# A kernel whose builder searches for its own instruction order: eight series of rounds in place of one

## The chip, the cores and the metric

The kernel runs on one core of a Trainium2 chip. The metric is the time in microseconds on the device. Before the change the median of three runs is 3045.0 us (3042.98 to 3045.96).

An order of instructions is fixed when the program is built. The time that the builder takes on the host is not part of the metric.

## The reference

The input is 64 graphs of 256 nodes with 256 features, and an adjacency matrix of 0 and 1 for each. Four layers follow one another; each normalizes, computes, and adds to `x`.

```python
h = jnp.maximum(_layernorm(x), 0.0); x = x + gat0(h, adj)   # layer 0
h = jnp.maximum(_layernorm(x), 0.0); x = x + gat1(h, adj)   # layer 1
h = jnp.maximum(_layernorm(x), 0.0); x = x + gat2(h, adj)   # layer 2
h = jnp.maximum(_layernorm(x), 0.0); x = x + ggnn(h, adj)   # layer 3
# gat0, gat1: 4 heads of 64; gat2: one head of 256
Wh = h @ W;  e = leaky_relu(Wh @ a_src [:, None] + Wh @ a_dst [None, :])
out = softmax(where(adj > 0, e, NEG)) @ Wh       # gat0: elu(out)
                                                 # gat1: relu(out + bias) + Wh, layer norm per head
# ggnn: three steps of a gated recurrent unit (GRU)
m = h @ weight[i];  aggr = adj.T @ m
r, z = sigmoid(aggr @ w_ih.T + h @ w_hh.T + b), ...;  n = tanh(i_n + r * h_n)
h = (1 - z) * n + z * h
```

## The kernel before

**Units.** The 64 graphs are cut into 33 units: graph 0 alone (unit 0), 31 pairs (units 1 to 31), graph 63 alone (unit 32). For each unit, `graphs` records the four layers as operations: `layer0`, `layer1`, `layer2`, `gru`. Nothing is issued at this point. Before the units comes a group of set-up work, numbered -1: loads of weights, score columns, the products of the GRU's input weights (`input_gates`, line 1033), and differences of weights that are stored to DRAM as `sd` (line 1073) and read back as `sw` by every pair in every GRU step (line 1611).

**What the lines in the profile are.** The attention layers use TensorE for transposes (line 1144), projections (1166), the spreading of scores in the first three units (1203) and the weighted sums (1275). The attention weights `pt` are made by ScalarE (1256) and VectorE; the latter goes through the helper at line 913, as most VectorE work does. `layer1` then has a chain of some ten VectorE steps for each half of the heads, with a power on GpSimd in it (1408, 1409) and the addition onto `xt` (1420). `norm` has statistics on VectorE (1109, 1110), a power on GpSimd (1118, 1119) and ScalarE's `xn` or `hn` (1127). The GRU has aggregations over the adjacency matrix (1471), products for pairs (1623, 1566), gates (1486) and transposes back (1501). SyncE issues the loads (1320, 1322), four DMA transposes of the mask per pair (1352), the broadcast of scores (1230), the `sw` loads (1611) and the stores (1703).

**Who sets the order.** `_Schedule` (from line 546 of the kernel) does. Each recorded operation has an engine, a cost in ns, the operations that it needs, and the buffers that it takes from pools of fixed size (5 of `xt`, 13 of `g`, 3 of `sw`, 8 PSUM banks and so on). Three of its methods matter here.

- `paths` gives every operation a first due time. It counts back from the end of the operation's unit, which lies at half of `PACE` = 93800 ns for each graph up to the unit's last.
- `play(due)` plays the program forward by the costs. An engine that is free takes, of the operations that have all they need, the one due first:

```python
heapq.heappush(able[o.engine], (due[o.index], o.index))
```

  It also gives out the buffers. It returns the order with its planned start times, the buffers taken, and the planned span.
- `latest(starts)` plays the program backward from the end, taking the operations in the reverse of the planned starts. What it returns is how late each operation could start; that is the next round's due times.

`run` lets `play` and `latest` alternate for seven rounds and keeps the order with the shortest planned span. It then issues every operation in that order, and each engine executes its instructions in the order issued. The same operations are issued whatever the order; what differs is their sequence on each engine, the buffers that they get, and so the waits between engines.

The costs stand in the code: for example 1725 for a GRU product of a pair, `dve(700)` less an overlap of 80 for a VectorE operation on 512 elements per partition, 485 less 80 for one on `pt`, 450 for any DMA issued by SyncE, 340 from TensorE's end to the start of another engine. `play` has one TensorE speed.

Of the kernel before, what the change touches and what calls it, by code (L numbers as in the profile page):

```python
# [2 lines left out]

# [542 lines left out]
class _Schedule:  # L546
# [11 lines left out]

    ENGINES = ("pe", "act", "dve", "pool", "sp")
    OVERLAP = {"pe": 0, "act": 90, "dve": 80, "pool": 0, "sp": 0}
    HOP = {"pe": 340, "act": 210, "dve": 210, "pool": 240, "sp": 0}
# [2 lines left out]
    DMA_AHEAD = 2000  # L566
    STRETCH = 3.43
    MARGIN = 1100
    ROUNDS = 7

    def __init__(self, tc, pools):

# [91 lines left out]
    def latest(self, starts):  # L664

        left = {o.index: len(o.succs) for o in self.ops}
        able = {e: [] for e in self.ENGINES}
        idle = dict.fromkeys(self.ENGINES, True)
        events, before_end = [], {}
# [8 lines left out]
        while True:  # L678
            for e in self.ENGINES:
                held = []  # L680
# [31 lines left out]
    def play(self, due):  # L712

        ops = self.ops
        able = {e: [] for e in self.ENGINES}
        idle = dict.fromkeys(self.ENGINES, True)
        waits = [len(o.preds) for o in ops]
# [26 lines left out]
        while True:  # L744
            for e in self.ENGINES:
                if not idle[e] or e == "sp" and dma_free > clock + self.DMA_AHEAD:
# [42 lines left out]
        return trace, slots, clock if done == len(ops) else float("inf")  # L789

    def run(self):
        due = self.paths()
        self.span = float("inf")
        for _ in range(self.ROUNDS):
            trace, slots, span = self.play(due)
            if span < self.span:
                self.trace, taken, self.span = trace, slots, span
            elif span == float("inf"):
                break
            due = self.latest({o.index: clock for clock, o in trace})  # L800
        assert self.span < float("inf")
        for _, o in self.trace:
            for b in o.takes:
                if b.tile is None:
                    b.slot = taken[b]
                    b.tile = self.pools[b.cls][0].tile(b.shape, b.dtype, name=f"{b.cls}{b.slot}")
            self.issue(o)
# [980 lines left out]
```

## Time and profile before

| what | value |
|---|---|
| median of the runs | 3045.0 us |
| the profiled execution | 3046.62 us |
| its span, first to last instruction | 3044.8 us |
| TensorE busy | 2974.3 us (98%) |
| TensorE loading weights | 2478.7 us (81%) |
| VectorE busy | 2606.7 us (86%) |
| ScalarE busy | 2124.8 us (70%) |
| GpSimd busy | 425.4 us (14%) |
| mean granted TensorE clock | 0.991 |

The profile is of one execution. "Busy" is the time in which an engine had an instruction under way. A view by windows cuts the span into stretches and gives the busy time of each engine in each, the granted TensorE clock and the DMA's share. A view of waits gives, for each engine, the time that it sat idle before instructions of a line, and which instruction let it go on. A timeline lists the instructions of one engine in order; what stands in square brackets is the idle time before the instruction and who ended it. An fp32 matmul is recorded as two.

### The profile page before, as it was taken

The numbers are of one execution on the slowest core, as the hardware profiler recorded it, in microseconds if no ns is written. First come the engines' busy times: TensorE is split into PE (matmuls) and PEld (weight loads), VectorE is DVE, ScalarE is ACT, GpSimd is POOL, SyncE is SP. The second block draws the span as 40 slices with busy tenths as digits, with TensorE's granted clock in tenths as the row PEclk, the third lists the DMA queues.
The fourth block names the chain that finished last, engine by engine and source line by source line (L and its number), as shares of the span: only waits on it lengthen the run. The fifth ranks groups of instructions, "written<-read, shape, count | busy, mean of one in ns | idle before, by whom it ended". The sixth has DMA issues, their size and how long they took to land.

```text
span 3044.8 us, 58325 instructions
## 1 busy us (share of the span) xinstructions
PE 2974.3 (98%) x21458; PEld 2478.7 (81%) x21458; DVE 2606.7 (86%) x6310; ACT 2124.8 (70%) x4997; POOL 425.4 (14%) x643
## 2 busy tenths in 40 slices
PE   8699999999999999999999999999999999999998
PEld 7588787888888888888888888888888888888887
DVE  7877788988988888988888988888988888988774
ACT  7566577776777776677777777777777777776554
POOL 3301101111111011111011111011111011111000
PEclk9799999999999999999999999999999999999999
DMA  5111122212212212212222222211222221211110
GB/s 146 40 62 44 55 81 78 81 54 84 74 64 84 84 54 80 74 65 83 84 67 69 72 67 84 84 70 64 70 70 81 84 72 62 67 63 59 49 42 28
DMA packets 150946, 212.56 MB, mean 70 GB/s; under 512 B 49238, under 2 KB 102012, under 8 KB 143228
## 3 DMA queue, kind: packets, MB, share of 16 engines
q1 hardware_dynamic: 146752, 207.40, 21.3%
q8 instruction: 172, 2.82, 0.4%
q10 hardware_dynamic: 3900, 1.34, 0.2%
q14 instruction: 122, 1.00, 0.1%
HBM read 180.62 MB, written 19.68 MB: 66 GB/s over the span
## 4 chain that ended last, share of the span: by engine, by line
PE 90%; DVE 6%; ACT 1%; DMA 1%; POOL 1%; SPq 1%; issue 0%; ACTq 0%; DVEq 0%; POOLq 0%
PE bank L1623 34%; PE bank L1486 12%; PE bank L1166 11%; PE bank L1275 11%; PE bank L1566 9%; PE bank L1471 6%; PE bank L1144 4%; PE bank L1501 3%; DVE o L913 1%; DVE g L913 1%; DVE pt L913 1%; SPq L1352 1%; PE bank L1203 1%; DMA sw<-sd 1%; ACT pt L1256 1%; DVE mean L913 0%
## 5 line engine op out<-in xcount | busy, mean ns | idle before, releaser
L913 ACT ACTIVATE g<-bank,bg 128x256 f32<-128x256 f32 (+1 forms) x780 | 395.3, 522 | 222.0 <-PE bank L1623 100.1
L1256 ACT ACTIVATE pt<-cb,f 128x256 f32<-128x256 f32 x1062 | 465.0, 504 | 99.9 <-PE bank L1275 99.6
L913 DVE SCALAR_TENSOR_TENSOR pt<-pt,f,cap 128x256 f32<-128x256 f32 x1152 | 487.7, 477 | 18.1 <-ACT pt L1256 12.8
L1275 PEld LDWEIGHTS bank<-wh,pt 128*64 128x64 f32 (+1 forms) x8704 | 347.7, 141 | 73.5 <-issue 46.7
L1275 PE MATMUL bank<-wh,pt 128*64 128x65 f32 (+1 forms) x8704 | 396.0, 232 | 7.5 <-DVE pt L913 6.7
L1486 PE MATMUL bank<-ag,wc 128*128 128x512 f32 (+1 forms) x888 | 383.1, 561 | 0.0
L913 ACT ACTIVATE g<-g,bg 128x256 f32<-128x256 f32 x570 | 267.1, 502 | 133.3 <-DVE g L913 105.2
L1623 PE MATMUL bank<-g,sw 128*128 128x256 f32 x1488 | 351.5, 379 | 0.0
L913 ACT COPY g<-bank 128x512 f32<-128x512 f32 x279 | 163.1, 585 | 252.0 <-PE bank L1623 234.3
L1623 PEld LDWEIGHTS bank<-g,sw 128*128 128x128 f32 x1488 | 282.7, 190 | 38.6
L1486 PEld LDWEIGHTS bank<-ag,wc 128*128 128x128 f32 x888 | 160.6, 190 | 106.9 <-issue 95.4
L1118 POOL TENSOR_SCALAR mv<-mv 128x4 f32<-128x4 f32 (+1 forms) x132 | 48.0, 364 | 1409.9 <-DVE mv L1110 1131.3
L1471 PE MATMUL bank<-am_r,hl 128*128 128x256 f32 x1536 | 235.1, 299 | 0.8 <-DVE am_r L913 0.4
L913 DVE TENSOR_TENSOR g<-bank,g 128x512 f32<-128x512 f32 x279 | 190.3, 683 | 37.4 <-PE bank L1623 20.7
L1127 ACT ACTIVATE xn<-xt,mv 128x256 f32<-128x256 f32 x384 | 208.9, 598 | 10.9 <-DVE mv L913 10.5
L1109 DVE BATCH_NORM_STATS2 st<-xt 128x6 f32<-128x256 f32 x512 | 208.6, 407 | 7.7 <-DMA xt<-in_x_dram 7.4
L1471 PEld LDWEIGHTS bank<-am_r,hl 128*128 128x128 f32 x1536 | 202.4, 189 | 10.6 <-DVE hl L913 1.1
L1623 PE MATMUL bank<-ag,sw 128*128 128x256 f32 x744 | 179.1, 384 | 7.7 <-DVE g L913 4.1
L1623 PE MATMUL bank<-ag,wc 128*128 128x256 f32 x744 | 179.4, 384 | 0.7 <-ACT ag L913 0.7
L1623 PE MATMUL bank<-ht,whh 128*128 128x256 f32 x744 | 178.7, 384 | 0.8 <-ACT ht L913 0.8
L1623 PE MATMUL bank<-g,s 128*128 128x256 f32 x744 | 176.1, 380 | 0.0
L1623 PE MATMUL bank<-g,wc 128*128 128x256 f32 x744 | 175.9, 379 | 0.0
(128 smaller groups left out, 5892.7 us busy)
## 6 DMA issues: line engine op xcount, KB each, us to landing
sw<-sd SPq DMA_DIRECT2D x279, 256.0 KB, 2.6
cb<-rd SPq DMA_DIRECT2D x58, 1024.0 KB, 4.6
xt<-in_x_dram SPq DMA_DIRECT2D x31, 512.0 KB, 3.7
at<-in_adj_dram SPq DMA_DIRECT2D x31, 512.0 KB, 6.0
out_dram<-xt SPq DMA_DIRECT2D x31, 512.0 KB, 3.0
cb<-rd SPq DMA_DIRECT2D x29, 256.0 KB, 3.3
sd<-g SPq DMA_DIRECT2D x9, 256.0 KB, 2.3
cap<-cap_n SPq DMA_TRANSPOSE x128, 2.4
```

Of the source, the lines that this page charges most:

```text
L913: emit = lambda: fn(*[a() if callable(a) else a for a in args], **kw)
L1109: nc.vector.bn_stats(st.tile[:, c, :], xt.tile[:, c, :])
L1127: op("act", 610, lambda: nc.scalar.activation(xn.tile[:, c, :], xt.tile[:, c, :], AF.Relu, bias=mv.tile[:, 3, c : c + 1], scale=mv.tile[:, ...
L1144: nc.tensor.transpose(ps.tile[:, c * P : (c + 1) * P], xn.tile[:, c, dc * P : (dc + 1) * P], ident)
L1166: nc.tensor.matmul(ps.tile[:, : heads * W], lhsT=ht.tile[:, dc, c * P : (c + 1) * P], rhs=we[:, dc].rearrange("p h w -> p (h w)"), start=( ...
L1256: op("act", 500, lambda: nc.scalar.activation(pt.tile[:, b, jc, :], source(h, b), AF.Exp, scale=slope - 1.0, bias=f.tile[:, 1, h, c : c + ...
L1275: nc.tensor.matmul(ps[q * Q : (q + 1) * Q], lhsT=pt.tile[:, b, jc, i0 : i0 + Q], rhs=wh.tile[:, h, 2 * b + jc, :w], start=(jc == 0), stop= ...
L1471: nc.tensor.matmul(ps.tile[:, b * N : (b + 1) * N], lhsT=hl.tile[:, k, 2 * b + sc, :], rhs=am.tile[:, 2 * b + sc, :], start=(k == 0 and sc ...
L1486: nc.tensor.matmul(ps.tile[:, :S], lhsT=w[:, dc, g * P : (g + 1) * P], rhs=v.tile[:, dc, :], start=(first and dc == 0), stop=(last and dc ...
L1501: nc.tensor.transpose(ps.tile[:, c * P : (c + 1) * P], ht.tile[:, j, c * P : (c + 1) * P], ident)
L1566: op("pe", 432, lambda: nc.tensor.matmul(ps.tile[:, where], lhsT=w, rhs=v(), start=first, stop=False, skip_group_check=True,), [*reads, B_ ...
L1623: nc.tensor.matmul(ps.tile[:, j * N : (j + 1) * N], lhsT=w()[:, dc, j * P : (j + 1) * P], rhs=view()[:, dc], start=(first and j == 0 and d ...
```

## The change

`run` searches in `KICKS` = 8 series of up to `ROUNDS` = 4 rounds each, in place of one series of seven. The first series starts from `paths`, as before. Each later series starts from `home`, the due times derived from the best order so far, with an offset added to whole groups: each group with a number below 6 is moved with a chance of 0.6, by an amount drawn from a normal distribution with a deviation of 30000 ns. Number -1 is below 6 as well, so the set-up work is among the groups that can move. The random numbers come from a fixed seed, so that the build always gives the same order. The order with the shortest planned span over all the series is issued.

```diff
+import random
...
-    ROUNDS = 7
+    ROUNDS = 4
+    KICKS = 8
+    SEED = 13
+    SHAKE = 30000.0
...
     def run(self):
-        due = self.paths()
+        home, close = self.paths(), float("inf")
         self.span = float("inf")
-        for _ in range(self.ROUNDS):
-            trace, slots, span = self.play(due)
-            if span < self.span:
-                self.trace, taken, self.span = trace, slots, span
-            elif span == float("inf"):
-                break
-            due = self.latest({o.index: clock for clock, o in trace})
+        rnd = random.Random(self.SEED)
+        groups = sorted({o.group for o in self.ops})
+        for kick in range(self.KICKS):
+
+            off = {g: rnd.gauss(0, self.SHAKE) if kick and g < 6 and rnd.random() < 0.6 else 0.0 for g in groups}
+            due = {o.index: home[o.index] + off[o.group] for o in self.ops}
+            for _ in range(self.ROUNDS):
+                trace, slots, span = self.play(due)
+                if span == float("inf"):
+                    break
+                due = self.latest({o.index: clock for clock, o in trace})
+                if span < close:
+                    home, close = due, span
+                if span < self.span:
+                    self.trace, taken, self.span = trace, slots, span
         assert self.span < float("inf")
```

No operation, cost, pool or dependency is touched.

## The prediction

> **What bounds the kernel now.** I read the page's first two parts, then the windows, then TensorE's waits in the stretch that the windows pointed to, then timelines of TensorE and SyncE. The page:
>
> ```profile
> span 3044.8 us, 58325 instructions
> PE 2974.3 (98%) x21458; PEld 2478.7 (81%) x21458; DVE 2606.7 (86%) x6310; ACT 2124.8 (70%) x4997; POOL 425.4 (14%) x643
> PE   8699999999999999999999999999999999999998
> PEclk9799999999999999999999999999999999999999
> ```
>
> TensorE is the bound: it idles 3044.8 - 2974.3 = 70.5 us. Of 40 slices only the first three and the last are below 9, and the granted clock drops in the second. Cut by stage (columns: span, then busy time and instructions of PE, PEld, DVE, ACT, POOL, then clock, DMA share, GB/s):
>
> ```profile
> 0.00:80.00 80.00, 65.66 (x718) 57.18 (x720) 58.04 (x184) 60.39 (x175) 23.25 (x49) 1.00 0.48 139
> 80.00:145.00 65.00, 41.02 (x376) 34.12 (x373) 54.78 (x162) 31.57 (x76) 20.54 (x25) 0.76 0.15 45
> 145.00:360.00 215.00, 201.99 (x1407) 170.17 (x1406) 170.57 (x422) 137.58 (x328) 33.26 (x46) 0.96 0.18 56
> 360.00:500.00 140.00, 135.58 (x1033) 111.44 (x1032) 118.50 (x291) 104.98 (x254) 17.06 (x26) 0.99 0.22 68
> 500.00:2960.00 2460.00, 2454.24 (x17568) 2042.16 (x17567) 2161.89 (x5170) 1754.85 (x4092) 330.05 (x495) 1.00 0.22 71
> 2960.00:3045.00 85.00, 75.80 (x372) 63.57 (x370) 42.94 (x89) 35.43 (x78) 1.21 (x2) 0.98 0.09 27
> ```
>
> Idle by stage: 14.3, 24.0, 13.0, 4.4, 5.8, 9.2 us. From 500 to 2960 us it is 0.2%: no order can win anything there, but one could lose. The start, 80 to 500, holds 41.4 us. The first 14.3 are nearly all the wait for the first input: the first matmul starts at 13.76. TensorE's waits in the first 250 us:
>
> ```profile
> PE bank L1144 <- ACT xn L1127: 30.6, 2, 16.8
> PE bank L1275 <- DVE pt L913: 6.7, 4, 3.8
> PE bank L1566 <- ACT ag L913: 5.1, 1, 5.1
> ```
>
> The 30.6 are the initial 13.8 and one stall of 16.8. In TensorE's timeline:
>
> ```profile
> 104.84 2.80 PE L1144 MATMUL bank<-ident,xn 128*128 128x128 f32 x8 [16.79 <-ACT xn L1127]
> 108.04 5.94 PE L1166 MATMUL bank<-w1e,ht 128*128 128x264 f32 x16 [0.40 <-ACT ht L913]
> ...
> 256.11 1.04 PE L1144 MATMUL bank<-ident,xn 128*128 128x128 f32 x8
> ```
>
> TensorE has done all it was given by 88 us (99% busy from 20 to 80) and waits until 105, while VectorE works off `layer1` chains of three units (18.1 us busy from 80 to 100). No GRU has begun: the first aggregation (line 1471) starts at 147 us, the first GRU product (1623) at 165. The eight transposes after the stall take 2.80 us where the same eight take 1.04 at 256 us.
>
> **What the Trainium skill says.** "TensorE: Matmul & The Clock Gate", Part 1 (The HAM clock gate): an idle window of about 3.4 us puts TensorE at half clock, and about as much steady work restores it. The trace agrees: stalls of 16.8, 3.85 and 5.07 us are each followed by doubled matmul times. "Perfetto Trace Analysis", Identifying the Most-Contended Engine: a busy matmul row says little of the room left, LDWEIGHTS busy says more. Here that is 81% and 98%; but GRU products are planned at 1725 ns and follow each other at 1.73 us on the chain of work, so between stalls there is no slack for an order to use. "DMA: Bandwidth & Descriptors", Issuing engines are not separate DMA queues: issue time is usually small beside the transfer. The four transposes of one pair disagree; they are used below.
>
> **The change part by part.** On the chip nothing is added or removed: the same operations, so 21458 matmuls and 6310 VectorE instructions stay, a few waits apart. What moves is their sequence, in the first six units and the set-up by intent, everywhere by consequence, since each round lays out the whole program anew.
>
> *More series.* Series one repeats the first four plays of before. If the order of before came from one of those, the planned span cannot get longer; if it came from play five to seven, the later series must first win that back. I do not know which. With 28 more plays around the best order I expect a shorter planned span.
>
> *The shake.* Seven groups (-1 to 5) move with a chance of 0.6, so some four per series, by about 24 us (0.8 x 30). That is the size of the fault: the 35 us from 73 to 108, in which VectorE serves three units before one is ready for its GRU. A unit brought forward would reach its GRU while TensorE now waits.
>
> *Does the plan tell the truth?* Costs beside the trace: two heads of weighted sums 1978 against 2.02 us; four projections 4 x 895 = 3580 against 3.56; VectorE on 512 elements 620 against 0.60 on the chain; `pt` 405 against 0.40. Where these rule, a stall saved in the plan is one saved on the chip. Two things the plan lacks. One is the clock: sequences after stalls against the same ones warm give +1.76 (1144), +2.2 (1166), +1.8 (1275), +0.9 (1144), +0.5 (1166) up to 145 us, +1.05, +0.8, +1.9, +0.5 near 235, +1.7 and +0.5 near 337: 13.6 us. A removed stall over 3.4 us returns some of this too. The other is SyncE:
>
> ```profile
> 873.70 5.78 SPq L1352 DMA_TRANSPOSE cap<-cap_n  x4
> 879.58 40.69 SPq L1611 DMA_DIRECT2D sw<-sd  x7
> ```
>
> Four transposes hold the queue for 5.78 us; the plan has 4 x 0.45 = 1.8. The `sw` load behind them starts 4 us late, lands 2.9 us after its issue, and TensorE takes it at once. TensorE waits on `sw` six times, 3.1 us in all.
>
> *Sum.* What can go is 41.4 idle, 13.6 of slow clock and perhaps 4 of the tail's 9.2: 59 us, a floor of 3044.8 - 59 = 2986. No engine's work forbids it: up to 360 us VectorE is busy 283.4 us. The chains of the units do forbid part. I take a third of idle and clock, (41.4 + 13.6) / 3 = 18.3, because seven draws of several offsets at once will seldom hit all three stalls. The bounds of this share are none (or below: next part) and all. Tail and middle I cost at nothing: the middle is hidden by a full TensorE, and its stalls in 2460 us are 5.8. If that cover went, each 0.2% of the middle would cost 5 us. So 3044.8 - 18.3 = 3026.5 of span; the execution profiled lasted 1.8 longer than its span, and 1.6 longer than the median, so the median should come at about 3027.
>
> After the stall at 88 us is filled, I expect the next late thing to be VectorE's feeding of the second and third GRU, where 230 (5.07 us) and 331 (2.6 and 1.1) are late now.
>
> **The rivals.** *(A) The large gain.* One unit reaches its GRU by about 90 us and TensorE never goes dry: the 16.8 stall, most of the other 24.6 and the slow clock go, 40 to 50 us, 2995 to 3005. For it: VectorE is busy only 113 of the first 145 us. Against: its work before the first GRU is serial, and GpSimd's power (1.3 to 2 us each) sits in it.
>
> *(B) No change.* The best order is that of before, or wins a few us in the plan in waits that the chip does not have (GpSimd's power is planned at 1600 and takes 1.3): 3039 to 3051, say 3045. For it: `latest` and `play` already ran seven rounds. Against: the first stall is plain in the very operations that the plan costs well.
>
> *(C) Slower, through SyncE's queue.* The new order puts the transposes just ahead of `sw` loads that TensorE needs soon. The plan sees 1.8 us and the chip takes 5.78, so up to 4 us of TensorE idle per pair, with up to 2 us of slow clock behind it where the idle passes 3.4. Today six waits cost 0.5 each. At 1 us in each of 31 pairs it is +31, less the gain of 18: 3058. It decides once the mean wait passes 18 / 31 = 0.6 us per pair. For it: the queue is in order and a late load is invisible to the plan. Against: three `sw` buffers let loads run ahead, and the queue waits 1571 us for TensorE to free them, so most are issued with nothing ahead of them.
>
> That the change does not do what it says is no further rival: an unhelpful shake falls under (B).
>
> **How the numbers follow.** Middle gain 0.50 (its own range 3012 to 3038), large gain 0.16, no change 0.13, slower 0.21. Within 0.2% is 6 us, about what a measurement of this kernel can tell. So faster 0.66, same 0.13, slower 0.21. The range reaches down to the better end of (A), leaving 0.04 below, and up past the mean of (C), leaving some 0.1 above: 2995 to 3060. The predicted time is that of the middle gain, 3027.
>
> **What would show it.** Right: the same instruction counts of TensorE and VectorE; TensorE's idle from 80 to 500 down from 41.4 to some 27; the wait of 1144 on `xn` below 30.6; the clock of the second slice above 0.7; the first aggregation before 147 us; 500 to 2960 still within 6 us of idle. (A) shows a first aggregation near 90 us and no stall over 3.4 us. (B) shows the same stall of 16.8, or another as long at another place. (C) shows a wait of line 1623 on `sw` in the tens of us, spread over the middle. I am wrong if the idle time moves from the start to the middle or the tail: the plan's best span may be bought there, with stalls that its costs make too short.

## The result

The changed kernel takes 3029.17 us (median of five runs, 3026.75 to 3031.41), beside 3045.0 us for the kernel before on the same chip. The ratio is 0.9949, with a 95% interval of 0.9935 to 0.9964: 15.5 us faster. Run again beside the experiments it took 3031.64 us against 3046.5, a ratio of 0.995 (0.9936 to 0.9963).

The page of the changed kernel. Its lines are numbered 13 higher than before: 1144 is 1157, 1623 is 1636.

```profile
span 3024.9 us, 58276 instructions
PE 2966.3 (98%) x21458; PEld 2474.1 (82%) x21458; DVE 2612.0 (86%) x6310; ACT 2125.7 (70%) x4997; POOL 430.0 (14%) x643
PE   7799999999999999999999999999999999999998
PEclk9999999999999999999999999999999999999999
```

The instruction counts of the five engines are those of before. TensorE's idle time is 3024.9 - 2966.3 = 58.6 us, where it was 70.5, and the dip of the clock in the second slice is gone. The windows, with the same cuts as before:

```profile
0.00:80.00 80.00, 63.55 (x724) 55.18 (x725) 60.38 (x189) 56.62 (x161) 21.85 (x45) 1.00 0.45 133
80.00:145.00 65.00, 49.73 (x416) 42.72 (x415) 62.03 (x179) 42.29 (x106) 25.09 (x35) 0.92 0.21 66
145.00:360.00 215.00, 207.50 (x1463) 174.81 (x1462) 174.62 (x434) 147.55 (x349) 31.59 (x43) 1.00 0.17 54
360.00:500.00 140.00, 133.97 (x1065) 110.17 (x1064) 117.10 (x287) 99.65 (x242) 20.89 (x30) 0.99 0.25 81
500.00:2960.00 2460.00, 2454.68 (x17514) 2042.78 (x17513) 2166.56 (x5158) 1753.58 (x4084) 330.60 (x490) 1.00 0.22 71
```

From 80 to 500 us TensorE idles 15.3 + 7.5 + 6.0 = 28.8 us, where it was 41.4. The time comes from 80 to 145 and from 145 to 360; from 360 to 500 it idles 1.6 us more. From 80 to 145 VectorE is busy 62.0 us where it was 54.8, so more of what TensorE waits for is worked off there. The middle idles 5.3 us (5.8 before). The first 80 us got worse, 16.5 against 14.3. TensorE's waits in the first 250 us, and two lines of its timeline:

```profile
PE bank L1157 <- ACT xn L1140: 23.5, 4, 15.1
PE bank L1288 <- POOL mv L1131: 5.0, 1, 5.0
PE bank L1157 <- ACT g L926: 2.9, 1, 2.9
```

```profile
95.23 1.94 PE L1157 MATMUL bank<-ident,xn 128*128 128x128 f32 x8 [8.04 <-ACT xn L1140]
...
129.17 3.64 PE L1288 MATMUL bank<-wh,pt 128*128 128x257 f32 x8 [5.03 <-POOL mv L1131]
```

The stall of 16.8 us at 88 us has become one of 8.04; the longest wait on `xn`, 15.1, is now the one for the first input (13.8 before). The first aggregation starts at 138.4 us, where it started at 147.3.

### The profile page after: what moved, and what is told of

Its sections match the earlier page's. It is cut to its first block, busy times and chain, and to the rows that moved or that the text cites. A ratio compares the mean times of both kernels' runs of the same rounds, so it can differ in the third digit from the quotient of the medians.

```text
span 3024.9 us, 58276 instructions
## 1 busy us (share of the span) xinstructions
PE 2966.3 (98%) x21458; PEld 2474.1 (82%) x21458; DVE 2612.0 (86%) x6310; ACT 2125.7 (70%) x4997; POOL 430.0 (14%) x643
## 4 chain that ended last, share of the span: by engine, by line
PE 88%; DVE 7%; ACT 1%; SPq 1%; POOL 1%; DMA 1%; issue 1%; ACTq 0%; DVEq 0%; POOLq 0%
PE bank L1636 34%; PE bank L1499 11%; PE bank L1179 11%; PE bank L1288 10%; PE bank L1579 9%; PE bank L1484 6%; PE bank L1157 3%; PE bank L1514 3%; DVE g L926 1%; DVE o L926 1%; DVE pt L926 1%; SPq L1365 1%; DVE st L1122 1%; DVE mean L926 0%; DVE xt L926 0%
## 5 line engine op out<-in xcount | busy, mean ns | idle before, releaser
L926 DVE SCALAR_TENSOR_TENSOR pt<-pt,f,cap 128x256 f32<-128x256 f32 x1152 | 489.8, 476 | 12.6 <-ACT pt L1269 8.9
```

Source lines behind the costliest of these rows:

```text
L926: emit = lambda: fn(*[a() if callable(a) else a for a in args], **kw)
```

## The experiments

Which of the shakes gave this order can be told by playing the plan through. The planned spans in us, one for each play, with the groups moved and by how much (the line of before has its seven rounds):

```
before:                                  3096.2 3058.4 3060.3 3071.9 3063.9 3070.9 3080.6
after, series 1, nothing moved           3096.2 3058.4 3060.3 3071.9
  2  -1: -18.0, 1: -41.8, 2: +12.9, ...  no complete order
  3  -1: +24.4, 2: -2.7                  3058.0 3043.5 3044.1 3069.8
  4  3: +16.7, 5: +1.2                   3071.4 3058.1 3059.7 3074.0
  5 to 8  three to six groups            3061.0 or worse (7: no complete order)
```

So the order of before came from the second play, and one shake of the seven gave that of after. Each experiment below is compared with the kernel before, run beside it on the same chip. The theory: the chip follows the plan's differences about one to one, through TensorE's idle time at the start. The rivals: the planned span says little about the chip; or the gain is TensorE's clock; or one half of the shake carries it by itself.

Most experiments replay one chosen order. Their edit is the same, with other steps each time; a step holds offsets in ns and a number of plays, and the last play's order is issued:

```diff
-    ROUNDS = 7
+    STEPS = [({}, 2), ({2: -2731.335503310831}, 3)]
...
     def run(self):
-        due = self.paths()
...
+        home = self.paths()
+        for off, plays in self.STEPS:
+            due = {o.index: home[o.index] + off.get(o.group, 0.0) for o in self.ops}
+            for _ in range(plays):
+                self.trace, taken, self.span = self.play(due)
+                due = self.latest({o.index: clock for clock, o in self.trace})
+            home = due
```

**One half of the shake: unit 2 alone** (the edit above).

> The order that one half of the winning shake gives: unit 2 moved by -2.7 us, the set-up not moved, third play. The builder plans a span of 3051.3 us for it, where it plans 3058.4 for the order of before and 3043.5 for that of after. Theory (the chip follows the plan's differences, about one to one): 7 us below before, 3034 to 3040. Rival (the planned span says little, any other order of the start lands where it will): no better placed than 3020 to 3060.

Measured: 3031.13 us, ratio 0.9949 (0.9935 to 0.9962). That is the whole gain of the change, twice what the plan promises for this order, and faster than the 3034 to 3040 that were expected. The windows from 80 to 360 us:

```profile
80.00:145.00 65.00, 46.80 (x444) 39.29 (x444) 62.65 (x184) 38.87 (x100) 24.24 (x29) 0.84 0.11 34
145.00:360.00 215.00, 205.06 (x1435) 170.87 (x1434) 171.25 (x425) 146.40 (x346) 32.66 (x45) 0.99 0.20 61
```

TensorE idles 28.1 us here (37.0 before, 22.8 after), and over the whole span 60.8, only 2.2 more than after. The direction was right and the size was not: the 7.8 us that the plan puts between this order and that of after are not there on the chip.

**The other half: the set-up alone.**

```diff
+    STEPS = [({}, 2), ({-1: 24424.666212141346}, 1)]
```

> The other half of the winning shake: the set-up moved by +24.4 us, unit 2 not moved, first play (the best of its series, planned at 3060.5 us, 2.1 above before). Theory (the chip follows the plan, and the gain is not in the set-up by itself): 3043 to 3052, no faster than before. Rival (moving the set-up out of the way of the first units is what wins): 3027 to 3036, as after.

Measured: 3050.86 us, ratio 1.0015 (1.0008 to 1.0021), slower by some 4.6 us; the plan says 2.1. TensorE's idle time is 72.8 us. Moving the set-up is not what wins; 2.7 us on unit 2 are enough.

**Another order with the planned span of before.**

```diff
+    STEPS = [({}, 2), ({-1: 24424.666212141346, 2: -2731.335503310831}, 2),
+             ({3: 16676.958607140805, 5: 1215.34822927822}, 2)]
```

> Another order with the planned span of before: the second play of the fourth series, planned at 3058.1 us (before 3058.4). Theory: as long as before within 5 us, 3040 to 3050, and TensorE's idle time up to 500 us again near 55. Rival (the plan says little): anything from 3020 to 3060.

Measured: 3042.03 us, ratio 0.9985 (0.9979 to 0.9992), 4.6 us below before. The time fell where the theory put it, within 5 us of before; since the rival allowed the same time, this run does not decide between them. The idle time did not fall where it was expected: 45.7 us up to 500, not 55. TensorE idles 7.3 us less than before in all and is busy 4.2 us longer.

**The order of the very first play.**

```diff
+    STEPS = [({}, 1)]
```

> The order of the very first play, before any search, planned at 3096.2 us, 37.8 above before. Theory: 30 to 50 us slower than before, 3075 to 3095, the more because stalls that are longer also cost clock. Rival: within 15 us of before.

Measured: 3100.26 us, ratio 1.0172 (1.0156 to 1.0187), 52 us slower where the plan says 37.8. The two longest waits of TensorE from 500 us on:

```profile
PE bank L1621 <- DMA sw<-sd: 29.9, 23, 2.0
PE bank L1499 <- DVE ht L911: 9.0, 5, 3.8
```

This is the prediction's rival (C) at full price: GRU products (line 1621 here) wait 23 times for an `sw` load, 1.3 us each, 29.9 us in all, where before has 3.1. The stretch from 500 to 2945 us idles 31.1 us. One of these waits beside SyncE's queue:

```profile
518.56 5.90 SPq L1350 DMA_TRANSPOSE cap<-cap_n  x4
525.14 6.78 SPq L1609 DMA_DIRECT2D sw<-sd  x3
529.61 1.97 PE L1621 MATMUL bank<-g,sw 128*128 128x256 f32 x8 [1.41 <-DMA sw<-sd]
```

The load stands behind four transposes that hold the queue for 5.90 us. The waits need not be the whole of what the plan lacks: TensorE is also busy 11.6 us longer than before (2985.9 against 2974.3), and `play` has one TensorE speed.

**The clock, first attempt: stalls filled with products.** In the order of before:

```diff
+    WARM = {968: 16, 274: 3, 807: 4, 1177: 2}
...
+        for _ in range(self.WARM.get(o.index, 0)):
+            self.fill(next(b for b in o.takes if b.cls == "bank"))
         o.emit()
...
+    sched.fill = lambda ps: nc.tensor.matmul(
+        ps.tile, lhsT=ident, rhs=whh[:, 0, :512], start=True, stop=True, skip_group_check=True)
```

> The order of before, with 25 extra fp32 products of the identity with 512 columns of a weight on TensorE (some 0.86 us each) just ahead of the four matmul groups that follow its long stalls (16, 3, 4 and 2 of them), written to the bank that the group then overwrites. They fill the stalls and move nothing else. Theory (of the 19.9 us that the change wins, 8.0 are the clock no longer dropping after stalls): 7 to 12 us below before, 3033 to 3038, with TensorE's clock in the second slice at 1.0. Rival (the doubled matmul times after a stall are a way of recording, and the gain is idle time alone): as before, 3042 to 3050, or above by what the products delay.

Measured: 3051.11 us, ratio 1.0015 (1.0008 to 1.0022), slower. TensorE's timeline:

```profile
98.31 15.46 PE L906 MATMUL bank<-whh,ident 128*128 128x512 f32 x32 [10.59 <-issue]
113.60 1.04 PE L1147 MATMUL bank<-ident,xn 128*128 128x128 f32 x8
114.88 3.87 PE L1169 MATMUL bank<-w1e,ht 128*128 128x264 f32 x16 [0.24 <-ACT ht L916]
118.59 1.04 PE L1147 MATMUL bank<-ident,xn 128*128 128x128 f32 x8
```

The products started only at 98.3, probably because the bank that they write came free then (the view names no instruction that released them). So the transposes behind them start 8.8 us later than before, at 113.60 in place of 104.84. But transposes and projections now take 1.04 and 3.87, where they took 2.80 and 5.94 behind the stall. From the start of these transposes to the start of the next ones pass 4.99 us, where 8.97 passed before (104.84 to 113.81): the doubling is time on the chip, not a way of recording. The end is 4.5 us later, less than the 8.8.

**The clock, second attempt.**

```diff
+    WARM = {968: 5, 274: 1}
```

> The order of before with 6 extra products instead of 25: 5 ahead of the transposes after the 16.8 us stall, 1 ahead of the weighted sums after the 3.85 us one. In the run with 25 their bank came free only 6.5 us before those transposes could start, so that 16 held them up by 9 us, but the transposes behind them took 1.04 in place of 2.80. Theory (time at the slow clock costs the end of the kernel what it costs on the spot): 4 to 8 us below before, 3038 to 3042. Rival (behind the stall TensorE is not what the next steps wait for, and its lost time vanishes in the next stall): within 3 us of before.

Measured: 3042.8 us, ratio 0.9992 (0.9983 to 1.0), 2.4 us below before with an interval from 5.2 to nothing. That is within the 3 us of the rival, but the interval reaches into the 4 to 8 us of the theory, so the run settles neither. Nor did the edit do what it was made for: five products did not keep TensorE at speed (the projections behind them still took 5.51 us). How much of the clock's loss reaches the end stays open.

**A longer search of the same kind**, replayed step by step:

```diff
+    STEPS = [({}, 2),
+             ({-1: 3584.7616253810434, 1: -1327.0898714969578, 3: -2087.8519832188113,
+               4: 17743.57342468822, 5: 3804.748202189743}, 3),
...
```

> The order that a longer search of the same kind gives: several hundred series with offsets of 3, 10 or 30 us deviation, planned at 3040.4 us, 3.1 below after and 18.0 below before. Theory (the chip follows the plan): 3 to 6 us below after, 3022 to 3026. Rival (the last few us of a plan picked as the best of many are not there on the chip, as the 7.8 us were not that lie between the plan of unit 2 alone and that of after): no faster than after, 3026 to 3036.

Measured: 3025.3 us, ratio 0.9932 (0.9918 to 0.9946). The plan says 18.0 below before, the chip 20.7. On the same chip this is 6.3 us below the changed kernel (3031.64, next run), and the five runs of each do not overlap: 3024.2 to 3027.4 against 3028.7 to 3033.4. So the last few us of this plan were there. TensorE idles 35.8 us up to 500, and 10.4 from there to 2945 (after: 5.3), with the `sw` waits up to 5.5:

```profile
PE bank L1621 <- DMA sw<-sd: 5.5, 8, 1.1
```

**The changed kernel beside it**, without an edit.

> The changed kernel once more, beside the others on one chip: 3026 to 3032, so that the half with unit 2 alone and the longer search are compared with it under the same conditions.

Measured: 3031.64 us, as stated above. Its profiled execution has a span of 3031.5 us, 6.6 more than the first one of the same kernel. TensorE idles 60.1 us against 58.6, and is busy 2971.4 us against 2966.3; the clock from 145 to 360 is 0.98 against 1.00.

**Two corrections of the plan: TensorE's clock and the transposes' issue.** A transpose is the one DMA of 64 KB, which the first condition picks out. The search had some 430 series; it was begun anew with these costs, so its steps differ too.

```diff
+        for o in self.ops:
+            if o.engine == "sp" and o.nbytes == 1 << 16:
+                o.cost = 1240
...
+                    cost = o.cost
+                    if e == "pe":
+                        if clock - pe_end > 3400:
+                            cold = 3000.0
+                        extra = min(cold, cost)
+                        cold -= extra
+                        cost += extra
+                        pe_end = clock + cost
-                    end = clock + o.cost - self.OVERLAP[e]
+                    end = clock + cost - self.OVERLAP[e]
```

> An order found with a plan that knows two more things of the chip: behind an idle time of TensorE of over 3.4 us, the next 3 us of its work take twice as long, and one DMA transpose holds SyncE for 1240 ns in place of 450. Some 430 series as in the longer search; planned at 3035.9 us by these costs. Theory (the plan's costs are near enough, and what it lacked were these two): below the longer search's 3025, 3012 to 3022, with fewer waits on the sw loads (below 3 us) and TensorE's clock at 0.95 or more from 80 to 145 us. Rival (what the longer search still wastes at the start is forced by the units' chains, and knowing the clock changes nothing): 3022 to 3032.

Measured: 3010.91 us, ratio 0.9882 (0.9865 to 0.9898): 36 us below before, 18 to 21 below after, and a little below the 3012 to 3022 that were expected. The page's first lines, and all of TensorE's waits from 500 to 2960 us:

```profile
span 3008.9 us, 58262 instructions
PE 2967.2 (99%) x21458; PEld 2475.7 (82%) x21458; DVE 2614.4 (87%) x6310; ACT 2127.0 (71%) x4997; POOL 425.3 (14%) x643
```

```profile
PE bank L1511 <- DVE ht L923: 1.4, 2, 1.2
PE bank L1511 <- ACT g L923: 0.7, 1, 0.7
```

The idle time is 41.7 us: 31.5 up to 500, 2.1 in the middle, 8.1 in the tail. Its busy time is that of after. Against the longer search it idles 12.4 us less, 8.3 of them from 500 to 2960 us and 4.3 up to 500. No wait on `sw` is left in this stretch. The expected clock did not come: 0.84 from 80 to 145 us.

**The transposes' issue alone** (the first three lines of the last diff, and a search of some 190 series):

> One of the two corrections alone: a DMA transpose planned at 1240 ns of SyncE, TensorE's clock not planned; found in some 190 series. Theory (the two corrections share the gain of the run before: the transposes take away the waits on the sw loads, some 5 us over the longer search's order, the clock and the head the rest): 3015 to 3022, waits on sw below 1 us from 500 us on. Rival (the transposes alone carry it): 3008 to 3014. Third way (the clock alone carries it): 3022 to 3030.

Measured: 3016.86 us, ratio 0.9901 (0.9885 to 0.9918), as shared gains would have it; the intervals of the two corrected searches overlap. Again no wait on `sw` from 500 us on. The longest two are now:

```profile
PE bank L1502 <- DVE ht L914: 3.0, 3, 1.6
PE bank L1487 <- DVE bank L914: 2.5, 1, 2.5
```

It beats the longer search without corrections with fewer than half its series. But the vanished waits on `sw`, 5.5 us there, explain little of it: other waits took their place, and from 500 to 2960 us TensorE idles 8.5 us here and 10.4 there. Of the 7.5 us between the two profiled spans 4.8 are busy time, no more than what two executions of one order show. Since all these searches drew different numbers, neither what the transposes' cost adds nor what the planned clock adds is separated from the luck of the draws.

## Why the prediction came out right

Predicted were 3027 us and 18 us of gain; measured were 3029.17 and 15.5.

**More series and a shorter plan.** Held. The open question, whether the order of before came from a late play, is answered: from the second.

**The shake.** The mechanism, denser VectorE work and an earlier first GRU, held: the first aggregation came 9 us earlier. The reason given for it did not. Offsets of 24 us were argued to matter because a 35 us stretch was at fault. In fact 2.7 us on one unit won 15.5 us, the 24.4 us on the set-up lost 4.6 by itself, and five of the seven shakes gave no better plan than that of before at any play. As far as seven shakes and the two halves of one can tell, a shake is a new draw in this search, more than a move in a known direction. One reading was wrong too: the first GRU product of before starts at 150.46 us, not at 165, where a later one waits; in the changed kernel it starts at 141.39.

**Does the plan tell the truth.** Held, with limits:

| order | plan against before, us | chip against before, us (95%) |
|---|---|---|
| after, second time | -14.9 | -15.2 (-19.5 to -11.3) |
| unit 2 alone | -7.1 | -15.5 (-19.8 to -11.6) |
| series 4 | -0.3 | -4.6 (-6.4 to -2.4) |
| set-up alone | +2.1 | +4.6 (2.4 to 6.4) |
| longer search | -18.0 | -20.7 (-25.0 to -16.5) |
| first play | +37.8 | +52.4 (47.5 to 57.0) |

(The chip's column is the ratio less one, times the median of before beside it.) The signs agree throughout. A single order lies up to 8 us off. The one that is 15 off has 26.8 us more of waits on `sw` than before, which the plan prices in part at most, and 11.6 us more of busy time, which it does not price; their shares are not separated.

**The sum.** Expected were 13.8 us of idle time and 4.5 of clock. In the first pair of profiles the idle time fell by 11.9 and the busy time by 8.0; in the second execution of after, by 10.4 and 2.9 against the same profile of before. From 80 to 500 us, for which the idle term stood, it fell by 12.6; the first 80 us, costed at nothing, lost 2.1. The clock term lies between what two executions of one order show. That the total came so near is in part luck: the share of a third was a judgement, and the searched orders run here gain from 4.6 us (series 4) to 20.7 (longer search) with the same costs.

**What is late next.** Wrong. I named the feeding of the second and third GRU, near 230 and 331 us. The wait of 5.07 us there is gone, though one of 2.9 us stands at 240; the longest after the first input are now 8.04 us at 87 and 5.03 at 124, still ahead of the first GRU. The step that failed is the assumption that one change of order fills the first stall and leaves the later ones.

**The rivals.** (A) did not come with this seed; even the best order found, at 3010.9, stays above its 2995 to 3005. (B) fell: the interval excludes no change. (C) did not decide here: 2.9 us of `sw` waits in 5 places, where the break-even was 0.6 us in each of 31 pairs. But its mechanism is real. The first play waits 29.9 us on `sw`; and the two searches whose plan knows how long transposes hold SyncE ended without any such wait from 500 us on. What that correction is worth in time stays open (3016.9 against 3025.3 for the longer search, one draw each).

## What to carry to other kernels

When an order is searched for by a plan, hold each of the plan's costs beside the trace before searching longer. One queue was planned at 450 ns for an issue that takes 1.2 us; the orders searched with that cost wait 2.5 to 5.5 us on the loads behind it from 500 us on, and those searched with 1240 ns do not wait on them. A search need not avoid what its plan does not price. And a plan's last few us are not to be trusted one order at a time: run the best few, and compare idle time by stage rather than one span.

## What was not expected of the hardware

**The clock fell without one long stall.** In the order with both corrections, TensorE's timeline shows:

```profile
85.10 0.57 PE L1285 MATMUL bank<-wh,pt 128*64 128x65 f32 x12 [0.91 <-DVE pt L923]
87.37 0.34 PE L1285 MATMUL bank<-wh,pt 128*64 128x65 f32 x4 [1.71 <-DVE pt L923]
88.28 2.36 PE L1285 MATMUL bank<-wh,pt 128*64 128x65 f32 x32 [0.57 <-DVE pt L923]
91.06 0.92 PE L1285 MATMUL bank<-wh,pt 128*64 128x65 f32 x12 [0.42 <-DVE pt L923]
92.16 2.60 PE L1154 MATMUL bank<-ident,xn 128*128 128x128 f32 x8 [0.18 <-DVE o L923]
```

No gap is longer than 1.71 us, yet the eight transposes at 92 us take 2.60 us, much as after a stall of 16.8 (2.80), where they take 1.04 at full clock. The windows show the granted clock, the third number from the end, fall to half near 88 us:

```profile
86.00:88.00 2.00, 0.34 (x4) 0.23 (x4) 2.00 (x5) 0.08 (x1) 1.58 (x2) 0.95 0.00 0
88.00:90.00 2.00, 1.72 (x28) 1.60 (x28) 2.00 (x6) 0.55 (x1) 0.56 (x2) 0.50 0.00 0
```

From 84 to 88 us TensorE is busy for 1.09 us of 4. Several short gaps among short matmuls did what one long gap does. The run with six extra products shows it again: its clock is 1.00 from 106 to 107 us and 0.50 from 108 to 109, though from 104 on no gap is longer than 0.97 us; TensorE is busy 1.75 us of the 3 from 104 to 107. The Trainium skill ("TensorE: Matmul & The Clock Gate", Part 1: The HAM clock gate) names an idle window of about 3.4 us as a condition; here the clock fell with no idle time that long. The prediction said that the profile of before agrees; it had itself counted slow matmuls near 337 us, where the longest gap ahead of them is 2.58. The plan with the clock, which looks for single gaps over 3.4 us, does not see this, which fits the 0.84 that it left there.

**One order, two busy times.** Two profiled executions of the changed kernel differ by 5.1 us in TensorE's busy time and by 1.5 in its idle time, with the clock at 1.00 or 0.98 in the same stretch. A difference of 5 us in busy time between two orders, each from one profile, is no finding.
